# A six-layer attention and MLP stack on one core: where the normalised x and q are transposed

## The chip, the core and the metric

The kernel runs on one core of a Trainium2 chip. The metric is device time in microseconds (us). The core's engines are TensorE (PE: matmuls, and transpositions as matmuls against an identity), VectorE (DVE), ScalarE (ACT), GpSimd (POOL) and SyncE (SP), which here issues every DMA. On-chip memory is SBUF, 128 partitions wide; PE writes to PSUM, of which a tile here is one of 8 banks of 128 x 512 f32.

## The reference

The input x is (8, 1024, 128). With `mod = silu(c) @ wmod` cut into six vectors per batch element, the reference computes, in f32:

```python
h = layernorm(x) * (1 + ca) + sa
for i in range(6):
    xn = layernorm(h, ln1_w[i], ln1_b[i])
    q, k, v = heads(xn @ wq[i]), heads(xn @ wk[i]), heads(xn @ wv[i])   # 8 heads of 16
    context = softmax_over_tokens(k).T @ v
    h = (softmax_over_features(q) @ context) @ wo[i] + bo[i] + h
    xn = layernorm(h, ln2_w[i], ln2_b[i])
    h = leaky(xn @ w1[i]) @ w2[i] + h                                   # 128 -> 512 -> 128
x = x + ga * h
g = layernorm(x) * (1 + cb) + sb
x = x + gb * fp4_linear(silu(fp4_linear(g, w_gate)) * fp4_linear(g, w_up), w_down)
```

`fp4_linear` rounds both operands to a 4-bit grid in blocks of 16 and multiplies. The attention has no token-by-token matrix: `context` is 16 x 16 per head.

## The kernel before

**Layout.** One batch element b (1024 tokens of 128 features) is an SBUF tile of 128 partitions x 1024 columns: partition p holds tokens 8p to 8p + 7, each a chunk of 128 columns. It is worked in two halves (H = 2) of four chunks (HC = 4, HW = 512 columns). Matmuls contract over the partitions, so a projection needs its input with features on the partitions; that is what the transpositions are for.

**Lanes.** Four batch elements are in work at a time (LANES = 4). Lane b % 4 has its own set of big tiles, known by tags: X (the residual), A, B, C, D, E, and x0 (the original x). A tag is used again and again within a layer, and a new use waits for the last readers of the old one.

**A layer** (`layer`, L936), 48 times in all (8 batch elements x 6):

- `normed` (L919) for the attention: `layernorm` (L624) takes the statistics of each chunk (DVE, L640 and L646), 1/sqrt by a logarithm and an exponential (ACT, L660, L665) with one step of refinement (DVE, L670 to L686), and applies them: two chunks of a half on DVE (L692) and two on ACT (L699), into xh (tag A). `transposed` (L712) makes four PE transpositions into one PSUM bank (L718), and ACT takes the bank to xT (tag B) while it multiplies by the norm's weight and adds its bias, which are per-partition columns there (L928).
- k: one 512-column matmul per half with wk as the stationary operand (L948), maximum over tokens (DVE, L955), exponential with its sum (ACT, L971). q: four 128-column matmuls per half with a chunk of xT as the stationary operand (L995), softmax over features (DVE L1004, L1011, ACT L1018, DVE L1024, L1031), and the last multiplication on POOL (L1036), into tag D.
- k is transposed back (L718, copy on ACT at L1047), xh and k are multiplied into a 128 x 128 matrix (L1058), which goes through wv, a head mask and wo into m (L1067 to L1099).
- q is transposed (L718) and copied by ACT to qT (L1118, tag B); with its chunks as the stationary operand, m gives the attention's output (L1125), which DVE adds to x (L1110).
- `normed` for the MLP: xh in tag C, xT in tag A. Then four 512-column matmuls per half with w1 (L1171), the leaky activation on ACT (L1180), 16 128-column matmuls per half with chunks of the hidden tile as the stationary operand (L1188), and another addition on DVE (L1110).

After layer 6 of a batch element comes `ffn` (L1201): normalisation and modulation, fp4 rounding on DVE, ACT and POOL (`fp4`, L725), gate and up matmuls (L1232), fp4 again, transpositions (L1288), the down projection (L1312), and stores of x.

**The order.** No engine picks its own order. Every operation above is a step of a plan (`Plan`, L84) with an engine, an estimated duration, what it reads and writes, and a latency per engine until others see its result (`LAT`, L87: 2.6 us for SP). Steps marked `port` and all steps of POOL are kept apart in the plan (L174, L198). `order` (L143) simulates all engines and picks, at each moment, the step that can start first, and among equals the one with the longest tail of work behind it plus a lead. Leads stand in a table per batch element and stage (`LEAD`, L290: column 0 the start, 1 to 6 the layers, 7 the FFN), and `TURNS` (L301) changes single leads at given plan times. While the plan sees PE idle, it puts a matmul of the identity with itself in the gap (`warm`, L1358). The result is a fixed order per engine, which the engine then runs in sequence, each instruction waiting for its inputs. DMAs are steps of SP and stand in SP's order in the same way.

Of the kernel before, what the change touches and what calls it, by code (L numbers as in the profile page):

```python
# [11 lines left out]
ALU = mybir.AluOpType  # L12
# [219 lines left out]
    return 0.1 + n * 1.78e-3  # L232


def mm(n):

    return 0.0115 + n * 1.654e-3
# [5 lines left out]


TRANSPOSE = 0.109


@with_exitstack
def kernel(
# [38 lines left out]


    LEAD = [  # L290
        [2405, 3996, 461, 247, -1202, -1296, -1300, -3196],
        [1413, 1593, 3441, 1928, -2207, 1189, 1781, -248],
        [366, -108, -1676, -2703, -3835, 1594, -2630, -2514],
        [-241, 558, -1413, 208, -413, 228, -5405, -156],
        [694, -3633, -2192, -2384, -870, -487, -1194, -1272],
        [-3687, 2479, 1403, 3083, -1193, -6, -811, -1034],
        [725, 1777, 204, -1637, -400, -327, -320, -670],
        [3404, 589, 1158, 1867, -7, -962, -419, -2719],
    ]

    TURNS = [  # L301
        (3, [(1, 0, -62)]),
        (27, [(3, 0, -535)]),
        (36, [(2, 1, -485)]),
        (39, [(3, 1, -531)]),
        (45, [(0, 2, 1516), (2, 1, -553)]),
        (48, [(2, 1, -544)]),
        (57, [(1, 1, 1518), (1, 2, 2846), (1, 3, 649)]),
        (75, [(1, 1, 1516)]),
        (90, [(1, 1, 773)]),  # L310
        (105, [(0, 3, 2919), (0, 4, 1470), (0, 5, 1376), (0, 7, -524)]),
        (120, [(0, 3, 2762), (2, 1, -721)]),
        (150, [(1, 2, -201)]),
        (165, [(2, 1, 797)]),
        (180, [(1, 2, 1215)]),
        (210, [(2, 2, 832)]),
        (225, [(3, 1, 914), (3, 6, -4315)]),
        (240, [(0, 5, 828)]),
        (255, [(0, 5, 2639), (0, 6, 2635)]),
        (270, [(2, 3, 156)]),  # L320
        (285, [(0, 7, 811), (1, 3, 64)]),
        (300, [(4, 0, -33)]),
        (315, [(2, 2, 1013), (4, 0, 939)]),
        (330, [(3, 2, 544)]),
        (345, [(0, 7, 348), (2, 3, -400)]),
        (360, [(0, 7, 811), (2, 3, 1746), (2, 4, -2375)]),
        (405, [(1, 4, -3784), (4, 1, -3690)]),
        (420, [(1, 4, -3786)]),
        (435, [(2, 4, -3941)]),
        (450, [(1, 4, -2313)]),  # L330
        (465, [(4, 1, -4514)]),
        (480, [(1, 5, 1477)]),
        (495, [(3, 5, 1525)]),
        (525, [(1, 5, 1515), (2, 5, 1254)]),
        (555, [(1, 7, 1337)]),
        (570, [(2, 5, 1311)]),
        (600, [(1, 7, 1342)]),
        (615, [(1, 7, 1337), (3, 6, -3519), (5, 2, 2464)]),
        (630, [(3, 7, 1425)]),
        (675, [(5, 1, 2181)]),  # L340
        (690, [(4, 1, -2521)]),
        (705, [(2, 7, -2804), (4, 2, -2786), (4, 3, -4487), (4, 7, -1958)]),
        (735, [(5, 2, 3162)]),
        (780, [(6, 1, 323)]),
        (795, [(2, 7, -2027)]),
        (810, [(3, 7, 2088), (5, 3, 1769)]),
        (825, [(4, 3, -2043)]),
        (840, [(5, 4, -2386), (7, 1, 210), (7, 2, 779)]),
        (870, [(4, 3, -2494)]),
        (885, [(7, 1, 493)]),  # L350
        (915, [(6, 2, 913)]),
        (930, [(4, 3, -1826), (4, 4, -1241)]),
        (945, [(5, 4, -2139), (5, 6, -1878)]),
        (975, [(6, 3, -2917)]),
        (1005, [(7, 4, -2167)]),
        (1020, [(5, 5, -1207)]),
        (1035, [(5, 5, -1166)]),
        (1065, [(7, 4, -1977)]),
        (1140, [(4, 6, -2161), (5, 6, -1912)]),
        (1155, [(4, 6, -1857)]),  # L360
        (1170, [(4, 7, -1928)]),
        (1245, [(5, 7, -1905)]),
        (1260, [(6, 7, -139)]),
        (1275, [(6, 6, -1635)]),
        (1305, [(5, 7, -1974), (7, 7, 205)]),
        (1320, [(6, 7, -143), (7, 6, -143)]),
        (1335, [(6, 7, 201)]),
        (1350, [(6, 7, 206), (7, 7, 207)]),
    ]
    LATE = 140.0  # L370
    NQ = 4
# [337 lines left out]
        if HV:  # L709
            add("DVE", HV * 0.256, apply_v, r=[*at(src, h), mv, rstd], w=[low], port=True)  # L710

    def transposed(src, h):  # L712

        t = Ps(psum)

        def go():
            for c in range(HC):
                nc.tensor.transpose(  # L718
                    t.ap()[:, c * P : (c + 1) * P], chunks(half(src, h))[:, c, :], ident
                )  # L720

        add("PE", HC * TRANSPOSE, go, r=at(src, h), w=[t])
        return t

    def fp4(src, parts, ncol, n, i, last="POOL"):  # L725

# [189 lines left out]
            )  # L916


    def normed(ln, x, which, to, l, params, n):  # L919


        xh, xT = big(ln, which, f"xh_{n}"), big(ln, to, f"xT_{n}")
        for h in range(H):
            layernorm(ln, xh, x, h, n)
            t = transposed(xh, h)
            add(
                "ACT", act(HW, 2),
                lambda t=t, h=h: nc.scalar.activation(  # L928
                    half(xT, h), t.ap(), AF.Identity,
                    bias=col(params + 1, l), scale=col(params, l),  # L930
                ),
                r=[t, "cols"], w=at(xT, h),
            )
        return xh, xT

    def layer(x, b, l, ln, mod):  # L936
        n = f"{b}_{l}"
        xh, xT = normed(ln, x, "A", "B", l, 0, f"a{n}")

        nmax = Buf(lanes_p, [P, H + 1], f"nmax{ln}", f"nmax_{n}", H + 1)  # L940
        ksum = Buf(lanes_p, [P, H + 1], f"ksum{ln}", f"ksum_{n}", H + 1)
# [47 lines left out]
        for h in range(H):  # L989
            tq = Ps(psum)  # L990
            hs = slice(h * NH, (h + 1) * NH)

            def qmm(tq=tq, h=h):
                for c in range(HC):
                    nc.tensor.matmul(  # L995
                        tq.ap()[:, c * D : (c + 1) * D], half(xT, h)[:, c * P : (c + 1) * P],
                        wq_sb[:, l, :], start=True, stop=True,
                    )

            add("PE", HC * mm(D), qmm, r=[*at(xT, h), ("wq", l)], w=[tq])  # L1000

            add(
                "DVE", vec(HW),
                lambda tq=tq, hs=hs: nc.vector.tensor_reduce(  # L1004
                    qmax.ap()[:, hs], heads(tq.ap()), axis=AX.X, op=ALU.max
                ),
                r=[tq], w=[qmax[h]],
            )
            add(
                "DVE", vec(HW),  # L1010
                lambda tq=tq, h=h, hs=hs: nc.vector.tensor_tensor(  # L1011
                    heads(half(q, h)), heads(tq.ap()), each(qmax.ap()[:, hs]), ALU.subtract
                ),
                r=[tq, qmax[h]], w=at(q, h),
            )
            add(
                "ACT", act(HW) + 0.06,
                lambda h=h: nc.scalar.activation(half(q, h), half(q, h), AF.Exp),  # L1018
                w=at(q, h), func="exp",
            )  # L1020

            add(
                "DVE", vec(HW),
                lambda h=h, hs=hs: nc.vector.tensor_reduce(  # L1024
                    qsum.ap()[:, hs], heads(half(q, h)), axis=AX.X, op=ALU.add
                ),
                r=at(q, h), w=[qsum[h]],
            )
            add(
                "DVE", 0.25,  # L1030
                lambda hs=hs: nc.vector.reciprocal(qsum.ap()[:, hs], qsum.ap()[:, hs]),  # L1031
                w=[qsum[h]],
            )
            add(
                "POOL", pool2(HW) + 0.06,
                lambda h=h, hs=hs: nc.gpsimd.tensor_tensor(  # L1036
                    heads(half(q, h)), heads(half(q, h)), each(qsum.ap()[:, hs]), ALU.mult
                ),
                r=[qsum[h]], w=at(q, h),
            )  # L1040

        k = big(ln, "E", f"k_{n}")
        for h in range(H):
            t = transposed(kT, h)
            add(
                "ACT", act(HW),
                lambda t=t, h=h: nc.scalar.copy(half(k, h), t.ap()), r=[t], w=at(k, h),  # L1047
            )
# [53 lines left out]
            ),  # L1102
            r=[tc_, ksum[H], ("mb", l)], w=[m],
        )
        qT = big(ln, "B", f"qT_{n}")

        def onto_x(t, h):
            add(
# [3 lines left out]
            )  # L1112

        for h in range(H):
            t = transposed(q, h)
            add(
                "ACT", act(HW),
                lambda t=t, h=h: nc.scalar.copy(half(qT, h), t.ap()), r=[t], w=at(qT, h),  # L1118
            )
        for h in range(H):  # L1120
            to = Ps(psum)

            def out_mm(to=to, h=h):
                for c in range(HC):
                    nc.tensor.matmul(  # L1125
                        to.ap()[:, c * D : (c + 1) * D], half(qT, h)[:, c * P : (c + 1) * P],
                        m.ap(), start=True, stop=True,
                    )

            add("PE", HC * mm(D), out_mm, r=[*at(qT, h), m], w=[to])  # L1130
            onto_x(to, h)

        _, xmT = normed(ln, x, "C", "A", l, 2, f"m{n}")
        if l == L - 1:


# [24 lines left out]
        for h in range(H):  # L1161
# [23 lines left out]
            def ymm(ty=ty, hidden=hidden):  # L1185
                for c in range(HC):
                    for j in range(NJ):
                        nc.tensor.matmul(  # L1188
                            ty.ap()[:, c * D : (c + 1) * D], hidden(j)[:, c * P : (c + 1) * P],
                            w2g.ap()[:, j, :] if l == L - 1 else w2_sb[:, l, j, :],  # L1190
                            start=(j == 0), stop=(j == NJ - 1),
                        )
# [227 lines left out]
```

## Time and profile before

| | |
|---|---|
| median of 3 runs | 1400.22 us (1399.84 to 1400.36) |
| profiled execution, first to last instruction | 1398.7 us |
| PE busy / its weight loads | 1388.0 / 1115.6 us |
| DVE, ACT, POOL busy | 1136.0, 967.6, 250.4 us |
| transpositions of xh (attention), q, xh (MLP), k: instructions of each | 384 |
| evictions with weight and bias, L928 | 192, 0.777 us each |
| copies of qT, L1118 | 96, 0.586 us each |
| DMA issues of SP, bytes moved | 104, 18.79 MB |

The profiled execution's own time is given by its span, the first row's runs were not profiled; what lies around the span in a run is the difference of the two, 1.5 us. Durations in the table are medians of single records. A record holds the time until an instruction's result has landed, so records on one engine overlap: where the work is dense, what an instruction takes from its engine is the time from its start to the next one's start. An f32 matmul is recorded as two passes, each with its own weight load (PEld); a transposition is one. In lines of the timeline the columns are start, length, engine, line, operation, tiles and how many instructions were merged. "Idle before" an instruction is time of its engine only.

### The profile page before, as it was taken

What the parts mean: (1) busy time and instruction counts of PE and PEld (TensorE: products, weight loads), DVE (VectorE), ACT (ScalarE), POOL (GpSimd) and SP (SyncE); (2) the same over time, 40 slices, a digit from 0 to 9 for tenths busy, and PEclk for the clock granted to TensorE, in tenths of its full rate; (3) what the DMA queues carried; (4) which work ended last, traced back from release to release, by engine and by line L of the source; (5) the groups of instructions that cost most, each with busy time, mean ns of one, the idle gap of its engine ahead of it and who ended that gap; (6) DMA issues with size and microseconds to landing.
All of it is one profiled execution on the core that took longest, in us unless ns stands there. A gap on an engine that the chain in (4) does not pass through costs nothing. (4 is left out here: it accounts for less than half of the span.)

```text
span 1398.7 us, 26324 instructions
## 1 busy us (share of the span) xinstructions
PE 1388.0 (99%) x9181; PEld 1115.6 (80%) x9181; DVE 1136.0 (81%) x4504; ACT 967.6 (69%) x2284; POOL 250.4 (18%) x216
## 2 busy tenths in 40 slices
PE   9999999999999999999999999999999999999999
PEld 7779778877888887877887788787877887888877
DVE  8998747689878674999899999675767576899997
ACT  6886756676676765677768767676667667677674
POOL 2312000022201010223121241011010022222332
PEclk9999999999999999999999999999999999999999
DMA  7100000000000000000000000000000000000001
GB/s 219 47 1 1 1 1 1 1 17 12 16 1 1 1 1 1 16 13 20 27 12 13 1 31 1 1 1 1 1 1 1 0 1 1 2 1 1 16 8 39
DMA packets 16437, 18.79 MB, mean 13 GB/s; under 512 B 1600, under 2 KB 10536, under 8 KB 16304
## 3 DMA queue, kind: packets, MB, share of 16 engines
q1 hardware_dynamic: 16304, 17.10, 3.9%
q8 instruction: 73, 1.20, 0.4%
q14 instruction: 60, 0.49, 0.1%
HBM read 12.88 MB, written 4.22 MB: 12 GB/s over the span
## 5 line engine op out<-in xcount | busy, mean ns | idle before, releaser
L1171 PE MATMUL ps<-xT_m,w_sb 128*128 128x512 f32 x768 | 351.5, 593 | 1.3 <-ACT g L1240 0.9
L1171 PEld LDWEIGHTS ps<-xT_m,w_sb 128*128 128x128 f32 x768 | 136.3, 190 | 126.5 <-issue 90.4
L1036 POOL TENSOR_TENSOR q<-q,qsum 128x512 f32<-128x512 f32 x96 | 101.7, 1070 | 703.0 <-DVE qsum L1031 312.8
L1110 DVE TENSOR_TENSOR x<-ps,x 128x512 f32<-128x512 f32 x192 | 130.1, 681 | 111.9 <-PE ps L1188 96.6
L995 PEld LDWEIGHTS ps<-wq_sb,xT_a 128*128 128x128 f32 x768 | 96.3, 192 | 25.8 <-issue 16.3
L699 ACT ACTIVATE xh_a<-x,shift_a,rstd_a 128x128 f32<-128x128 f32 x192 | 83.4, 489 | 26.0 <-DVE shift_a L686 25.5
L1188 PEld LDWEIGHTS ps<-w_sb,hT_D 128*128 128x128 f32 x640 | 86.8, 192 | 15.8 <-issue 13.2
L995 PE MATMUL ps<-wq_sb,xT_a 128*128 128x128 f32 x768 | 98.6, 275 | 0.0
L1188 PE MATMUL ps<-w_sb,hT_E 128*128 128x128 f32 x640 | 97.6, 275 | 0.0
L1188 PE MATMUL ps<-w_sb,hT_C 128*128 128x128 f32 x640 | 97.6, 275 | 0.0
L1188 PE MATMUL ps<-w_sb,hT_B 128*128 128x128 f32 x640 | 97.6, 275 | 0.0
L1188 PE MATMUL ps<-w_sb,hT_D 128*128 128x128 f32 x640 | 97.5, 275 | 0.0
L1125 PEld LDWEIGHTS ps<-m,qT 128*128 128x128 f32 x768 | 91.4, 192 | 6.4 <-issue 1.4
L948 PE MATMUL ps<-xT_a,wk_sb 128*128 128x512 f32 x192 | 95.5, 596 | 0.5 <-DVE stats_a L640 0.3
L1058 PEld LDWEIGHTS ps<-k,xh_a 128*128 128x128 f32 x768 | 90.7, 192 | 6.4 <-issue 4.3
L1125 PE MATMUL ps<-m,qT 128*128 128x128 f32 x768 | 94.9, 275 | 0.0
L1058 PE MATMUL ps<-k,xh_a 128*128 128x128 f32 x768 | 93.4, 275 | 0.0
L699 ACT ACTIVATE xh_m<-x,shift_m,rstd_m 128x128 f32<-128x128 f32 x192 | 81.3, 487 | 17.3 <-DVE shift_m L686 17.1
L660 ACT ACTIVATE rstd_a<-mv_a,eps 128x4 f32<-128x4 f32 x96 | 28.4, 300 | 92.2 <-DVE mv_a L646 79.6
L640 DVE BATCH_NORM_STATS2 stats_a<-x 128x6 f32<-128x128 f32 x384 | 85.0, 278 | 1.6
L928 ACT ACTIVATE xT_m<-ps,cols 128x512 f32<-128x512 f32 x96 | 72.4, 777 | 19.9 <-PE ps L718 19.7
L1188 PEld LDWEIGHTS ps<-w_sb,hT_B 128*128 128x128 f32 x640 | 84.5, 192 | 0.7 <-issue 0.5
(181 smaller groups left out, 3217.8 us busy)
## 6 DMA issues: line engine op xcount, KB each, us to landing
x<-in_L_attn_x_dram SPq DMA_DIRECT2D x16, 256.0 KB, 3.2
out_dram<-x SPq DMA_DIRECT2D x14, 256.0 KB, 2.0
w_sb<-in_L_attn_w_dram SPq DMA_DIRECT2D x12, 256.0 KB, 4.5
mod<-mod_d SPq DMA_DIRECT2D x8, 256.0 KB
mod<-mod_d SPq DMA_DIRECT2D x4, 128.0 KB
out_dram<-x SPq DMA_DIRECT2D x4, 128.0 KB, 1.8
wk_sb<-in_L_attn_wk_dram SPq DMA_DIRECT2D x6, 64.0 KB, 3.4
wq_sb<-in_L_attn_wq_dram SPq DMA_DIRECT2D x6, 64.0 KB, 2.9
```

The lines of the kernel that those rows point to most:

```text
L640: "DVE", 0.197, lambda c=c: nc.vector.bn_stats(stats.ap()[:, c, :], s(c)),
L660: lambda: nc.scalar.activation(y(), var(), AF.Ln, bias=eps),
L699: nc.scalar.activation(d(c), s(c), AF.Identity, bias=shift.ap()[:, c : c + 1], scale=rstd.ap()[:, c : c + 1],)
L928: lambda t=t, h=h: nc.scalar.activation(half(xT, h), t.ap(), AF.Identity, bias=col(params + 1, l), scale=col(params, l),),
L948: lambda tk=tk, h=h: nc.tensor.matmul(tk.ap(), wk_sb[:, l, :], half(xT, h), start=True, stop=True),
L995: nc.tensor.matmul(tq.ap()[:, c * D : (c + 1) * D], half(xT, h)[:, c * P : (c + 1) * P], wq_sb[:, l, :], start=True, stop=True,)
L1036: lambda h=h, hs=hs: nc.gpsimd.tensor_tensor(heads(half(q, h)), heads(half(q, h)), each(qsum.ap()[:, hs]), ALU.mult),
L1058: nc.tensor.matmul(tc_.ap()[:, :D], chunks(xh.ap())[:, c, :], chunks(k.ap())[:, c, :], start=(c == 0), stop=(c == C - 1),)
L1110: lambda: nc.vector.tensor_tensor(half(x, h), t.ap(), half(x, h), ALU.add),
L1125: nc.tensor.matmul(to.ap()[:, c * D : (c + 1) * D], half(qT, h)[:, c * P : (c + 1) * P], m.ap(), start=True, stop=True,)
L1171: lambda th=th, h=h, j=j: nc.tensor.matmul(th.ap(), w1_sb[:, l, j * P : (j + 1) * P], half(xmT, h), start=True, stop=True,),
L1188: nc.tensor.matmul(ty.ap()[:, c * D : (c + 1) * D], hidden(j)[:, c * P : (c + 1) * P], w2g.ap()[:, j, :] if l == L - 1 else w2_sb[:, l, j, :],
```

## The change

For all layers but the first one of batch elements 0 to 3 (`dma = l > 0 or b >= LANES`), the transpositions of xh (attention), q and xh (MLP) go another way:

- one DVE instruction per half turns 32 x 32 blocks: partition block g keeps its partitions, and feature i*4 + f of token j of the block goes to partition i and column f*128 + j*4 + c (`turned`). It reads and writes with a step of four elements;
- four DMAs of SP, one per partition block, copy 32 partitions x 512 columns onto 128 partitions x 128 columns, in runs of 512 bytes, SBUF to SBUF, and finish the transposition: the column is now t*4 + c for token row t and chunk c;
- the norm's weight and bias, which ACT applied on the way out of PSUM, are applied in place on POOL (`tensor_scalar`); q has none.

The intermediate tile takes tag D before q, tag B for q, and tag B again for the MLP; the turned q is copied back into its own tile.

Columns within a half are therefore interleaved, t*4 + c in place of c*128 + t. Where PE takes one chunk's columns as the stationary operand (q, the transposition of k, the attention's output, the second MLP matmul) it now takes every fourth column (`each_chunk`).

In `normed`, in all 48 layers, the application of the statistics goes wholly to ACT (`layernorm(..., 0)`): four chunks of a half at L699, none at L692. `LEAD` and `TURNS` are replaced; the plan has three new constants for the new steps.

```diff
+def pool1(n):
+    return 0.1 + n * 1.2e-3
...
+TURN = 1.17e-3
+SQ = 32
...
     LEAD = [
-        [2405, 3996, 461, 247, -1202, -1296, -1300, -3196],
...
+        [6669, 6853, 111, 1873, 506, 0, 1316, 0],
...
     TURNS = [
-        (3, [(1, 0, -62)]),
...
+        (0, [(0, 1, 46), (0, 2, 3659), (2, 0, -210), (4, 6, 6661), (5, 2, -7325)]),
...
-    def transposed(src, h):
+    def each_chunk(t):
+        return t.rearrange("p (t c) -> p c t", c=HC)
+
+    def transposed(src, h, cut=chunks):
...
-                    t.ap()[:, c * P : (c + 1) * P], chunks(half(src, h))[:, c, :], ident
+                    t.ap()[:, c * P : (c + 1) * P], cut(half(src, h))[:, c, :], ident
...
+    def turned(src, via, dst, h):
+        add(
+            "DVE", TURN * HC * D,
+            lambda: nc.vector.transpose(
+                half(via, h).rearrange("p (f j c) -> p c f j", f=P // SQ, c=HC),
+                half(src, h).rearrange("p (c i f) -> p c f i", f=P // SQ, c=HC),
+            ),
+            r=at(src, h), w=at(via, h),
+        )
+
+        def spread():
+            for g in range(P // SQ):
+                nc.sync.dma_start(
+                    half(dst, h)[:, g * P : (g + 1) * P],
+                    half(via, h)[g * SQ : (g + 1) * SQ, :],
+                )
+
+        add("SP", P // SQ * 0.48, spread, r=at(via, h), w=at(dst, h))
...
-    def normed(ln, x, which, to, l, params, n):
+    def normed(ln, x, which, via, to, l, params, n, dma):
         xh, xT = big(ln, which, f"xh_{n}"), big(ln, to, f"xT_{n}")
+        y = big(ln, via, f"y_{n}") if dma else None
         for h in range(H):
-            layernorm(ln, xh, x, h, n)
-            t = transposed(xh, h)
-            add("ACT", act(HW, 2), ...)
+            layernorm(ln, xh, x, h, n, 0)
+            if not dma:
...
+                continue
+            turned(xh, y, xT, h)
+            add(
+                "POOL", pool1(HW),
+                lambda h=h: nc.gpsimd.tensor_scalar(
+                    half(xT, h), half(xT, h), col(params, l), col(params + 1, l),
+                    ALU.mult, ALU.add,
+                ),
+                r=["cols"], w=at(xT, h),
+            )
...
-        xh, xT = normed(ln, x, "A", "B", l, 0, f"a{n}")
+        dma = l > 0 or b >= LANES
+        cut = each_chunk if dma else chunks
+        xh, xT = normed(ln, x, "A", "D", "B", l, 0, f"a{n}", dma)
...
-                        tq.ap()[:, c * D : (c + 1) * D], half(xT, h)[:, c * P : (c + 1) * P],
+                        tq.ap()[:, c * D : (c + 1) * D], cut(half(xT, h))[:, c, :],
...
-            t = transposed(kT, h)
+            t = transposed(kT, h, cut)
...
-        qT = big(ln, "B", f"qT_{n}")
+        y = big(ln, "B", f"yq_{n}")
+        qT = q if dma else y
...
+            if dma:
+                turned(q, y, q, h)
+                continue
...
-                        to.ap()[:, c * D : (c + 1) * D], half(qT, h)[:, c * P : (c + 1) * P],
+                        to.ap()[:, c * D : (c + 1) * D], cut(half(qT, h))[:, c, :],
...
-        _, xmT = normed(ln, x, "C", "A", l, 2, f"m{n}")
+        _, xmT = normed(ln, x, "C", "B", "A", l, 2, f"m{n}", dma)
...
-                            ty.ap()[:, c * D : (c + 1) * D], hidden(j)[:, c * P : (c + 1) * P],
+                            ty.ap()[:, c * D : (c + 1) * D], cut(hidden(j))[:, c, :],
```

## The prediction

> **What bounds the kernel now.** I read the busy table first, then the 100 us windows, the timeline, the groups by line and the DMA issues.
>
> ```profile
> span 1398.7 us, 26324 instructions
> PE 1388.0 (99%) x9181; PEld 1115.6 (80%) x9181; DVE 1136.0 (81%) x4504; ACT 967.6 (69%) x2284; POOL 250.4 (18%) x216
> ...
> PE 38%; DVE 2%; ACT 0%; issue 0%; POOL 0%; ACTq 0%
> ```
>
> TensorE (PE) is busy for 1388 of 1398.7 us. The chain that ended last is followed back over two fifths of the span, and 38 of its 40 hundredths are PE. VectorE (DVE) is next at 81%. The filler matmuls of L1360 are 24.3 us of PE's time (174 instructions) and lie in the first 50 and the last 50 us, so between those PE is full of real work. The windows (start:length, then PE, PEld, DVE, ACT, POOL) say what happens when DVE is crowded too:
>
> ```profile
> 0.00:100.00 100.00, 95.35 (x616) 75.66 (x617) 94.04 (x464) 75.67 (x206) 25.76 (x31) 1.00 0.31 94
> ...
> 700.00:800.00 100.00, 100.00 (x645) 79.83 (x644) 92.77 (x340) 72.57 (x164) 23.62 (x19) 1.00 0.04 9
> ...
> 1000.00:1100.00 100.00, 100.00 (x640) 77.64 (x640) 63.63 (x268) 65.82 (x151) 8.40 (x8) 1.00 0.00 1
> ```
>
> With DVE at 93% PE still had no gap; DVE's other 19% is slack. So PE work taken away is time gained, until another engine is the later one. The clock was 1.00 throughout.
>
> What PE pays is the distance between starts, not the record, since records overlap:
>
> ```profile
> 699.65 0.60 PE L718 MATMUL ps<-ident,xh_a 128*128 128x128 f32 x4
> 700.09 0.61 PE L1188 MATMUL ps<-w2g,hT_B 128*128 128x128 f32 x4
> 700.53 0.61 PE L1188 MATMUL ps<-w2g,hT_C 128*128 128x128 f32 x4
> ```
>
> Four transpositions take 700.09 - 699.65 = 0.44 us, 0.109 each. A 128-column matmul is two passes of 0.111.
>
> **PE.** 44 of the 48 layers change (the first layer of lanes 0 to 3 does not), with two halves and three turns (xh for attention, q, xh for the MLP): 264 turns, each in place of four transpositions. 1056 x 0.109 = 115.1 us leave PE.
>
> **ACT.** Removed: 176 evictions of L928 at 0.663 us from start to start (116.7) and 88 copies of L1118 at 0.477 (42.0). Added: the other half of the norm's application, 384 chunks of L699 at 0.385 (147.8; all 48 layers). Net -11 us of 968: no change.
>
> **DVE.** The same 384 chunks leave L692: 98 us at the usual 0.256 from start to start, 121.5 with the stalls in its records; I take 110. The 264 turns of 128x512 come in.
>
> ```profile
> 699.59 0.68 DVE L903 TENSOR_TENSOR h<-h,mod 128x512 f32<-128x512 f32 x1
> 700.18 0.87 DVE L640 BATCH_NORM_STATS2 stats_a<-x 128x6 f32<-128x128 f32 x4
> 700.97 0.36 DVE L646 BATCH_NORM_AGGREGATE mv_a<-stats_a 128x2 f32<-128x6 f32 x4
> ```
>
> No row shows a turn, or a DVE stream that steps 16 bytes. The lower end is the ordinary 512-column operation, 700.18 - 699.59 = 0.59. The upper end is the slower statistics, 0.79 for four times 128 columns. An instruction can't cost less than nothing, and a gain is excluded. I take 0.60, the row of the same shape: 264 x 0.60 = 158 (upper end 209). DVE becomes 1136 - 110 + 158 = 1184 us (upper end 1235).
>
> A rule speaks against this. The Trainium skill, "VectorE: DVE Perf Modes", section "Rules for kernel authors", says to transpose 128x128 on TensorE where PSUM will do, and section "The three transpose paths" gives 390 ns there against 311 on VectorE, in bf16 and 32x32 blocks only. The trace's 0.109 in a stream is far under 390. An estimate by the page's 311 for each of four chunks is 1.24 us a turn and DVE at 1353, which would leave almost no gain.
>
> **POOL.** 176 scale-and-shift operations on 128x512 that ACT did in its eviction. Lower end: the memset of 768 columns took 0.742, so 0.50. Upper end: the two-input multiply, L1036, 1.07. I take 0.9, nearer the upper as the only 512-column row: 158 us, POOL 408, a third of the span. Behind one that waits stand the q multiplies (L1036), the FFN's L791 and the adds of L911, whose readers are DVE and PE. L692 went up to 1.3 us beside POOL work; fewer DVE chunks and more POOL work about cancel there.
>
> **SP and the copies.** Each turn issues four copies of 64 KB: 1056.
>
> ```profile
> 25.25 0.43 SPq L426 DMA_DIRECT2D wq_sb<-in_L_attn_wq_dram  x1
> 25.73 0.43 SPq L426 DMA_DIRECT2D wv_sb<-in_L_attn_wv_dram  x1
> ```
>
> The issues by line give the time to landing at the end:
>
> ```profile
> out_dram<-x SPq DMA_DIRECT2D x14, 256.0 KB, 2.0
> ...
> wq_sb<-in_L_attn_wq_dram SPq DMA_DIRECT2D x6, 64.0 KB, 2.9
> ```
>
> One issue takes 0.475 (25.73 - 25.25): 1056 x 0.475 = 502 us of SP, which has only 104 issues now. Packets of 512 bytes took 28.7 ns on average (7648 in the trace): 1056 x 128 x 28.7 / 16 = 242 us on each DMA engine, under a fifth of the span. Neither is a bound. On SP a turn that waits for DVE holds back the other lanes' copies, the loads of x and the stores.
>
> **Latency.** Before, xh to xT was 0.44 + 0.78 (eviction record) = 1.2 us. After: 0.60 for the turn, 3 x 0.475 until the fourth issue, 2.0 to 2.9 to land (no row copies SBUF to SBUF; I take 2.9), 0.9 on POOL: 5.8, so +4.6. q has no POOL step behind the copy: 4.9 against 1.0, +3.9. The cover is the time that data now wait for PE. As means over 96 halves, from the end of the eviction to the start of the first matmul, that is 2.5 us (xT for k), 6.5 (xT for w1) and 6.6 (qT). Two of three are covered; the first lacks 2.1. Four independent lanes share PE, so in the rewritten order another lane's matmul can stand there. If none did, 88 x 2.1 = 185 us would come back.
>
> **PE's strided weights.** Because columns now lie as t*4+c, the weight loads of the q, output and second MLP matmuls (48 per layer, two passes each: 4224 passes) and of k's transpositions (352) step 16 bytes. No row steps so. Loads now:
>
> ```profile
> 699.54 0.47 PEld L718 LDWEIGHTS ps<-ident,xh_a 128*128 128x128 f32 x4
> 699.98 0.53 PEld L1188 LDWEIGHTS ps<-w2g,hT_B 128*128 128x128 f32 x4
> ```
>
> A load takes 0.141 for a transposition and 0.192 for a matmul, and starts with the pass before it. The lower end is nothing, if the step is free (a gain is excluded: no column fewer is loaded). The upper end by rows is the spread of the two, 0.051 on each of 4576 passes: 233 us. I take nothing: every load is started a whole pass ahead, and both kinds keep the 0.11 between starts.
>
> The Trainium skill speaks against this too: "SBUF — State Buffer", "Specifications (TRN2)", has 16-byte lines that need two hits each for full speed, and here every element is on a new line. With the 128 / 1.2 = 107 ns that "TensorE: Matmul & The Clock Gate", "LDWEIGHTS", gives a load, halving the rate is an estimate of 4224 x 0.10 = 430 us more. No run here shows it.
>
> **The sum.** 1398.7 - 115.1 = 1283.6 if PE stays full. DVE would stand at 1184 / 1284 = 92%, as in the window 700:800, where PE lost nothing, and under the 94% of 0:100, where it lost 5% (start-up loads included). I take 2%, 26 us. Span 1309.6. The median of the runs, 1400.22, lies 1.5 above the profiled span, so the time is **1311**. Its own range is 1278 (no loss; POOL and DVE at their lower ends) to 1335 (4% loss).
>
> **The rivals.**
>
> *DVE or the copies come last* (0.27). For: DVE at 92% in the mean must go above that beside an FFN, whose windows already show 92 to 93%; and a third of the 185 us above is 62. Against: PE's fullness at 93%. With turns at 0.79, DVE's 1235 at 92% is 1342, so about 1345; with a third of the stalls, about 1350 as well. The turn cancels the gain from about 1.1 us (1026 + 264 x 1.1 = 1316, 94% of 1400); 0.02 of the chance lies near there, 0.07 beyond it.
>
> *Strided weight loads slow PE* (0.18), the case that ends slower. The place is the 48 matmuls per layer of L995, L1125 and L1188, the price up to 233 us: 1283.6 + 233 + 1.5 = 1518. It decides from 115 / 4576 = 25 ns per pass. For: nothing hides a load that outlasts its pass, and these are half of PE's time. Against: each is started a pass ahead, and a transposition's load, as many columns, takes only 0.141.
>
> *More than the sum* (0.02): under 1278, if DVE's lost stalls free PE as well.
>
> **Numbers.** Likeliest case 0.53. Faster: 0.53 + 0.02 + 0.18 of the first rival = 0.73. Same (within 0.2%, about what a measurement of this kernel can tell): 0.02 + 0.01 = 0.03. Slower: 0.07 + 0.17 = 0.24. The range runs from 1278 to 1455: it holds the likeliest case, nearly all of the first rival, and the second where the loads cost up to 37 ns. Some 0.16 lies outside.
>
> **What would show it.** PE: 1056 transpositions fewer, those that are left at 0.109; q, output and second MLP passes still 0.111 from start to start (the second rival: longer there, PE still at 99%). DVE: turns of 0.60 from start to start, busy about 1184. SP: four issues a turn, landing under 3 us. First rival: PE's idle time grows and is ended by POOL's xT or DVE. I am wrong on the mechanism if a strided pass is longer, and on the size if PE waits over 50 us.

## The result and the profile after

The changed kernel takes 1890.16 us in the median (1887.1 to 1890.86, 4 runs), the kernel before 1400.29 beside it (1399.84 to 1400.75). The ratio is 1.349, 95% interval 1.347 to 1.351: 490 us slower, where the forecast was 89 us faster. The profiled span is 1888.3 us, with a mean granted clock of 0.99. The head of the page and the first line of its chain:

```profile
span 1888.3 us, 28098 instructions
...
PE 1858.2 (98%) x8651; PEld 1585.5 (84%) x8651; DVE 1313.8 (70%) x4384; ACT 972.2 (51%) x2412; POOL 390.6 (21%) x392
...
PE 87%; DVE 8%; ACT 2%; issue 1%; DMA 1%; SPq 1%; POOL 1%; DVEq 0%; POOLq 0%; ACTq 0%
```

PE is about as full as before (98% for 99%), with 530 instructions fewer, and has 470 us more of work. So nearly all of the time went into longer instructions and not into waiting. The 100 us windows of the prediction (columns as there) say the same:

```profile
0.00:100.00 100.00, 95.60 (x618) 79.11 (x619) 87.01 (x412) 77.24 (x215) 28.87 (x35) 1.00 0.36 104
700.00:800.00 100.00, 98.51 (x452) 85.10 (x452) 71.59 (x231) 51.39 (x123) 24.56 (x22) 1.00 0.14 36
1000.00:1100.00 100.00, 99.31 (x500) 88.97 (x500) 70.38 (x240) 48.50 (x126) 21.40 (x22) 1.00 0.21 48
```

From 1000 to 1100 us PE is 99% busy, but with 500 matmul records where there were 640. Which ones grew, the timeline of PE shows (start, length):

```profile
757.51 1.10 PE L1266 MATMUL ps<-w_sb,hT_B 128*128 128x128 f32 x4
758.45 1.10 PE L1266 MATMUL ps<-w_sb,hT_C 128*128 128x128 f32 x4
759.38 1.10 PE L1266 MATMUL ps<-w_sb,hT_B 128*128 128x128 f32 x4
```

Four passes of the second MLP matmul now take 758.45 - 757.51 = 0.94 us; before it was 0.44. As medians from start to start over the whole trace, a pass with a strided stationary operand takes 0.233 us instead of 0.112, at all three places (L1069, L1203, L1266); k's transposition 0.120 instead of 0.109; a pass whose operand lies side by side 0.112, as before. The groups by line show it as weight loads, and show the turn:

```profile
L1069 PEld LDWEIGHTS ps<-wq_sb,xT_a 128*128 128x128 f32 x768 | 179.2, 316 | 11.4 <-issue 5.5 <-PE ps L1069 0.7 <-DVE shift_a L710 0.2
...
L1203 PEld LDWEIGHTS ps<-m,q 128*128 128x128 f32 x704 | 169.2, 328 | 12.5 <-DVE m L1173 5.6 <-issue 4.2 <-DVE stats_a L675 1.0
...
L1266 PEld LDWEIGHTS ps<-w_sb,hT_C 128*128 128x128 f32 x640 | 156.8, 316 | 0.0
L769 DVE STREAM_TRANSPOSE y_a<-xh_a 128x512 f32<-128x512 f32 x88 | 100.4, 1143 | 27.7 <-ACT xh_a L734 27.7
...
L1438 PE MATMUL warm<-ident 128*128 128x128 f32 x700 | 96.7, 282 | 2.4 <-POOL ident masks.py:199 1.6 <-DVE g L1326 0.5
...
L1000 POOL TENSOR_SCALAR xT_a<-xT_a,cols 128x512 f32<-128x512 f32 x88 | 70.3, 799 | 435.8 <-DMA xT_a<-y_a 339.9 <-PE ps L1203 40.2 <-ACT rstd_a L700 27.8
```

The fourth field is busy time and the mean of one record: loads of 328 ns where all are strided (316 where the four first layers, which do not change, are in the mean; 192 before), turns of 1143 ns, GpSimd operations of 799 ns, and 700 filler records where there were 174.

The sum of these terms closes: 1398.7 - 115 (1056 transpositions) + 511 (4224 strided passes x 0.121) + 4 (352 of k x 0.011) + 72 (fillers, 24.3 to 96.7) + 19 (PE's idle, 10.7 to 30.1) = 1890, against a span of 1888.3.

### The profile page after: what moved, and what is told of

Same layout as the page of the kernel before. It is cut to its first block, busy times and chain, and to the rows that moved or that the text cites. A ratio compares the mean times of both kernels' runs of the same rounds, so it can differ in the third digit from the quotient of the medians.

```text
span 1888.3 us, 28098 instructions
## 1 busy us (share of the span) xinstructions
PE 1858.2 (98%) x8651; PEld 1585.5 (84%) x8651; DVE 1313.8 (70%) x4384; ACT 972.2 (51%) x2412; POOL 390.6 (21%) x392
## 3 DMA queue, kind: packets, MB, share of 16 engines
q8 instruction: 70, 1.15, 0.3%
## 4 chain that ended last, share of the span: by engine, by line
PE 87%; DVE 8%; ACT 2%; issue 1%; DMA 1%; SPq 1%; POOL 1%; DVEq 0%; POOLq 0%; ACTq 0%
PE ps L1266 35%; PE ps L1249 16%; PE ps L1203 9%; PE ps L1069 8%; PE ps L1022 4%; PE ps L1132 4%; PE ps L757 2%; PE ps L1310 2%; PE warm L1438 2%; PE ps L1390 2%; PE ps L1366 1%; SPq L778 1%; ACT xh_a L734 1%; PE ps L1166 1%; DVE yq L769 1%
## 5 line engine op out<-in xcount | busy, mean ns | idle before, releaser
L1069 PEld LDWEIGHTS ps<-wq_sb,xT_a 128*128 128x128 f32 x768 | 179.2, 316 | 11.4 <-issue 5.5
L1203 PEld LDWEIGHTS ps<-m,q 128*128 128x128 f32 x704 | 169.2, 328 | 12.5 <-DVE m L1173 5.6
L1069 PE MATMUL ps<-wq_sb,xT_a 128*128 128x128 f32 x768 | 179.2, 383 | 0.0
L734 ACT ACTIVATE xh_a<-x,shift_a,rstd_a 128x128 f32<-128x128 f32 x384 | 157.3, 483 | 41.1 <-DVE shift_a L721 35.1
L1203 PE MATMUL ps<-m,q 128*128 128x128 f32 x704 | 171.6, 396 | 2.7 <-issue 1.4
L734 ACT ACTIVATE xh_m<-x,shift_m,rstd_m 128x128 f32<-128x128 f32 x384 | 155.4, 484 | 27.4 <-DVE shift_m L721 27.0
L1266 PE MATMUL ps<-w_sb,hT_E 128*128 128x128 f32 x640 | 167.9, 385 | 0.0
L1266 PE MATMUL ps<-w_sb,hT_C 128*128 128x128 f32 x640 | 167.9, 385 | 0.0
L1266 PE MATMUL ps<-w_sb,hT_B 128*128 128x128 f32 x640 | 167.0, 384 | 0.0
L1266 PEld LDWEIGHTS ps<-w_sb,hT_D 128*128 128x128 f32 x640 | 158.3, 314 | 10.3 <-issue 4.5
L1266 PE MATMUL ps<-w_sb,hT_D 128*128 128x128 f32 x640 | 164.6, 380 | 0.0
L1266 PEld LDWEIGHTS ps<-w_sb,hT_B 128*128 128x128 f32 x640 | 157.2, 315 | 3.0 <-issue 1.9
L1266 PEld LDWEIGHTS ps<-w_sb,hT_E 128*128 128x128 f32 x640 | 156.9, 316 | 0.0
L1266 PEld LDWEIGHTS ps<-w_sb,hT_C 128*128 128x128 f32 x640 | 156.8, 316 | 0.0
```

Source lines behind the costliest of these rows:

```text
L734: nc.scalar.activation(d(c), s(c), AF.Identity, bias=shift.ap()[:, c : c + 1], scale=rstd.ap()[:, c : c + 1],)
L1069: nc.tensor.matmul(tq.ap()[:, c * D : (c + 1) * D], cut(half(xT, h))[:, c, :], wq_sb[:, l, :], start=True, stop=True,)
L1203: nc.tensor.matmul(to.ap()[:, c * D : (c + 1) * D], cut(half(qT, h))[:, c, :], m.ap(), start=True, stop=True,)
L1266: nc.tensor.matmul(ty.ap()[:, c * D : (c + 1) * D], cut(hidden(j))[:, c, :], w2g.ap()[:, j, :] if l == L - 1 else w2_sb[:, l, j, :], start ...
```

## The experiments

Two theories for the step at first. **A**: the step of 16 bytes of the stationary operand makes each weight load, and with it each pass, longer. **B**: PE's operand reads suffer from what the change adds beside them, the copies above all. And a question behind both: does the forecast hold without the step?

**e1_contig.** The change with stationary operands side by side; the copies, turns and order stay.

```diff
-        cut = each_chunk if dma else chunks
+        cut = chunks
```

> The changed kernel with one edit: PE takes each chunk's 128 columns side by side again where the change takes every fourth one (the tokens come out in another order, so the output is not the reference's; turns, copies, POOL work and the order of all engines stay). Theory A (the step of 16 bytes slows the weight loads): the passes of the q, output and second MLP matmuls go from 0.233 us back to 0.112, 4224 x 0.121 = 511 us less, about 1380 us, DVE near 94% of the span. Rival B (PE is slow because of the copies or the traffic beside it): the passes stay near 0.233 and the time near 1890. Rival C (passes recover, but DVE, whose turns take 1.07 us, or the copies end last): passes 0.112, PE idle or on filler matmuls for over 100 us, time 1420 to 1500.

1456.63 us (1451.64 to 1459.86), ratio 1.039 (1.036 to 1.042). Passes are back at 0.112 with the copies still there, as theory A has it, and 434 of the 490 us are gone. But the rest is slower than the kernel before, not faster. Head and chain of the page:

```profile
span 1456.4 us, 27949 instructions
...
PE 1379.6 (95%) x8651; PEld 1076.3 (74%) x8651; DVE 1293.5 (89%) x4384; ACT 966.5 (66%) x2412; POOL 391.7 (27%) x392
...
DVE 48%; PE 30%; ACT 7%; DMA 5%; SPq 4%; issue 3%; POOL 2%; DVEq 0%; ACTq 0%; POOLq 0%
```

Now VectorE leads the chain, and the copies' queue and landing stand in it with 9 hundredths.

**e2_before_step4** and **e3_before_mixed**: the kernel before, with nothing added but the step of the stationary operand, by `every(t, c, s)`, which takes 128 columns with step s. In e2 it is 4 at q, k's transposition, the output and the second MLP matmul. In e3 it is 2 at q and k, 3 at the output, 1 at the MLP.

```diff
-                        tq.ap()[:, c * D : (c + 1) * D], half(xT, h)[:, c * P : (c + 1) * P],
+                        tq.ap()[:, c * D : (c + 1) * D], every(half(xT, h), c, 4),
```

> The kernel before with one edit: the stationary operands of q, the transposition of k, the attention's output and the second MLP matmul take every fourth column, in all 48 layers (a part of the computation is permuted, the output is not the reference's). No turn, no copy, no other order. Theory A: 4608 passes at 0.233 in place of 0.112 (558 us) and 384 transpositions at 0.120 in place of 0.109 (4 us): about 1960 us. Rival B (copies or traffic slow the loads): no change, 1400 us, passes at 0.112.

> The kernel before with steps of its own per line: q takes every second column (8 bytes), the attention's output every third (12 bytes), the transposition of k every second, the second MLP matmul stays at one (a part of the computation is permuted, the output is not the reference's). If a step costs as the lines of 16 bytes say, two hits in a line are enough: q passes stay at 0.112, the output's go up (4/3 hits a line) to between 0.15 and 0.23, and the time is 1430 to 1490. If any step costs the whole price: q and output at 0.233, 1536 x 0.121 = 186 us, about 1586. If only 16 bytes do: 1400.

e2 took 1946.25 us (one run), with passes of 0.233 and no copy or turn in the kernel: theory B falls. Two of its groups of four passes, and the output's loads:

```profile
699.88 1.10 PE L1194 MATMUL ps<-w_sb,hT_B 128*128 128x128 f32 x4
700.81 1.10 PE L1194 MATMUL ps<-w_sb,hT_C 128*128 128x128 f32 x4
```

```profile
L1131 PEld LDWEIGHTS ps<-m,qT 128*128 128x128 f32 x768 | 184.3, 328 | 5.0 <-DVE m L1105 0.9 <-ACT xT_m L934 0.5 <-ACT xh_m L699 0.5
```

e3 took 1453.25 (one run). Its weight loads by line (the output with step 3, q with 2, the MLP with 1, k with 2):

```profile
L1131 PEld LDWEIGHTS ps<-m,qT 128*128 128x128 f32 x768 | 139.2, 261 | 5.6 <-issue 1.1 <-DVE m L1105 0.9 <-ACT xT_m L934 0.5
...
L1001 PEld LDWEIGHTS ps<-wq_sb,xT_a 128*128 128x128 f32 x768 | 101.0, 196 | 25.5 <-issue 16.2 <-PE ps L1001 1.9 <-PE ps L954 1.4
...
L1194 PEld LDWEIGHTS ps<-w_sb,hT_D 128*128 128x128 f32 x640 | 86.9, 192 | 15.8 <-issue 12.4 <-ACT hT_B L1186 1.2 <-ACT k L1053 0.2
...
L724 PEld LDWEIGHTS ps<-ident,kT 128*128 128x128 f32 x384 | 52.0, 206 | 7.1 <-issue 3.7 <-ACT kT L977 2.1 <-DVE stats_i L640 0.2
```

From start to start a matmul's pass takes 0.112 us at step 1, 0.118 at 2, 0.174 at 3 and, in e2, 0.233 at 4. A step of 8 bytes is nearly free for it, one of 16 doubles the pass. k's transposition does not follow this: it takes 0.120 at step 2 and 0.121 at step 4 (0.109 at 1), and its load grows from 141 ns to 206 already at step 2.

**e4_turns** and **e5_free**: e1 with the turn's step taken away too. In e4 the attention's turn reads and writes side by side, the MLP's still reads with the step, q's still writes with it. In e5 all three are side by side; the edit below is e5's.

```diff
-                half(via, h).rearrange("p (f j c) -> p c f j", f=P // SQ, c=HC),
-                half(src, h).rearrange("p (c i f) -> p c f i", f=P // SQ, c=HC),
+                half(via, h).rearrange("p (c f j) -> p c f j", f=P // SQ, c=HC),
+                half(src, h).rearrange("p (c f i) -> p c f i", f=P // SQ, c=HC),
```

> E1 with three kinds of turn (data come out in another order): xh of the attention reads and writes side by side, xh of the MLP reads every fourth column and writes side by side, q reads side by side and writes every fourth (now all read and write with a step of four and take 1.07 us from start to start, 1.14 as records). Theory A2 (the turn itself takes two cycles an element): all three keep 1.14. Theory A3 (the step costs, as on PE): the first takes about 0.68 (0.60 from start to start); the second and third show which side costs, 1.14 or 0.68. Time under A3: DVE loses 88 to 264 x 0.47 us, 40 to 120, and the kernel 0 to 60 us against E1.

> E1 with turns that read and write side by side in all three places (blocks of 32 come out in another order, so the output is not the reference's): neither PE nor DVE steps 16 bytes any more; order, copies and POOL work are those of the changed kernel. The prediction's sum without the two steps is 1311. Theory D (what is left in E1 over that sum is DVE, which ends last): turns at 0.70 a record take another 79 us off DVE's busy time against E4, and the time falls from 1427 by about 0.75 of that, to 1365 to 1375. Theory L (the copies' latency and the order, which has filler matmuls written into it, hold PE up): DVE's relief helps little more, 1395 to 1415, with PE's 700 fillers and its idle time as in E4.

e4 took 1426.89 us (one run). Its turns:

```profile
L771 DVE STREAM_TRANSPOSE y_m<-xh_m 128x512 f32<-128x512 f32 x88 | 97.6, 1110 | 22.7 <-ACT xh_m L734 20.6 <-DMA xT_a<-y_a 1.5 <-DMA q<-yq 0.2
...
L771 DVE STREAM_TRANSPOSE yq<-q 128x512 f32<-128x512 f32 x88 | 97.4, 1122 | 3.1 <-POOL q L1112 2.8
...
L771 DVE STREAM_TRANSPOSE y_a<-xh_a 128x512 f32<-128x512 f32 x88 | 61.7, 702 | 25.7 <-ACT xh_a L734 25.6
```

The step on either side alone costs nearly the price of both. From start to start a turn takes 0.625 us side by side, 0.96 when only written with the step, 1.03 when read with it (1.02 to 1.03 in the change). e5 took 1407.64 (1405.44 to 1409.39), ratio 1.005 (1.003 to 1.007), with these busy times:

```profile
PE 1357.2 (97%) x8651; PEld 1072.7 (76%) x8651; DVE 1197.5 (85%) x4384; ACT 963.6 (69%) x2412; POOL 389.9 (28%) x392
```

So even with no step anywhere the change gives nothing: 97 us lie between e5 and the forecast's 1311.

**e7_no_copies, e8_no_fillers, e9_neither** ask what those are made of, with e5's order of all steps kept.

```diff
-                half(via, h).rearrange("p (c f j) -> p c f j", f=P // SQ, c=HC),
+                half(src, h).rearrange("p (c f j) -> p c f j", f=P // SQ, c=HC),
...
-        add("SP", P // SQ * 0.48, spread, r=at(via, h), w=at(dst, h))
+        add("SP", P // SQ * 0.48, lambda: None, r=at(via, h), w=at(dst, h))
...
-                    half(xT, h), half(xT, h), col(params, l), col(params + 1, l),
+                    half(xT, h), half(xh, h), col(params, l), col(params + 1, l),
```

(e7 and e9; in e8 and e9 the plan leaves a gap without a filler after its first 60 us.)

> The kernel of e5_free without its 1056 copies: the turns work in place, GpSimd reads the turned half directly and writes xT, the output matmul reads the turned q directly. The order on every engine and the 700 filler records stay as they are, so no step stands elsewhere. (Left out: the copies, so the result is not the reference's.) e5_free took 1407.6 with PE's records at 1357 of 1405.7, 97 of that fillers. If the copies' way (three further issues, 2.1 us to landing) makes PE wait: PE's idle 48 us falls below 20, time 1365 to 1380. If VectorE's load or the fixed order makes it wait: no change, 1398 to 1410.

> The kernel of e5_free without the filler matmuls after the first 60 us of the plan (568 of 700 records, about 79 us of PE's busy time); nothing else stands elsewhere. If fillers only fill waits that are there anyway: time 1400 to 1410, PE's idle grows from 48 to about 125 us. If fillers are themselves in the way, because real work is ready earlier than the plan thought: up to 79 us less, 1330 to 1390. The granted clock shows whether gaps cost clock: it stays at 1.00 if they do not.

> e7 and e8 together: no copies and no fillers after the first 60 us, order as in e5_free (result not the reference's). The PE work left is about 1260 + 18 us. If copies and fillers are what separates e5_free from the sum of the prediction (1311): 1285 to 1330. If VectorE (1197 us busy in e5_free) or the order still makes PE wait: 1345 to 1400.

e7: 1378.61 (1378.02 to 1380.41); e8: 1411.0 (1410.58 to 1411.67); e9: 1380.8 (1378.8 to 1381.68). Busy times of e7, then of e8:

```profile
PE 1347.8 (98%) x8651; PEld 1066.8 (77%) x8651; DVE 1190.7 (87%) x4384; ACT 962.2 (70%) x2412; POOL 387.9 (28%) x392
```

```profile
PE 1312.7 (93%) x8083; PEld 1014.5 (72%) x8083; DVE 1195.7 (85%) x4384; ACT 963.0 (68%) x2412; POOL 391.0 (28%) x392
```

The copies' way is worth 29 us. Leaving the fillers out gains nothing: e8 is 3 us slower than e5. PE idles for 96.1 us in place of 48.5, and its other records take 1293.7 us (1312.7 less the 19.0 of the fillers that stay) in place of 1260.2 (1357.2 less 97.0), with a mean granted clock of 0.978 for 0.993. So the fillers stand for the most part where PE would wait anyway. Whether some of them also hold up work that is ready is not shown, because the lower clock changes the same sum.

**e6_short_runs.** The change done in full without any step: the turn side by side on both sides, the copies in runs of 128 bytes to the right place, and the order of features that follows taken up by row-permuted loads of wk, wq and w1, in layers 1 to 5 of all batch elements. Leads as in the change.

```diff
-                half(via, h).rearrange("p (f j c) -> p c f j", f=P // SQ, c=HC),
-                half(src, h).rearrange("p (c i f) -> p c f i", f=P // SQ, c=HC),
+                half(via, h).rearrange("p (f c j) -> p c f j", f=P // SQ, c=HC),
+                half(src, h).rearrange("p (c f i) -> p c f i", f=P // SQ, c=HC),
...
-                    half(dst, h)[:, g * P : (g + 1) * P],
+                    chunks(half(dst, h))[:, :, g * SQ : (g + 1) * SQ],
```

> A kernel that computes the whole reference with turns in layers 2 to 6 of every batch element and no step of 16 bytes anywhere: the turn reads and writes side by side, the copies write runs of 128 bytes in place of 512 (four times as many packets), columns come out in their plain order, and the features' order on the partitions (i*4 + f for feature f*32 + i) is met by loading wk, wq and w1 in that row order and by permuting wk's columns, the head mask and the norm's columns once. Leads are those of the changed kernel, which were not made for it. Theory: turns 0.70 a record, passes 0.112, copies land within 4 us in spite of the short runs; the time itself is set by the order and lies between 1400 and 1480. Rival: 540 thousand packets of 128 bytes fill the DMA engines (over 60% of their time) and the landings go over 6 us, 1500 or more.

1479.62 us (one run); passes 0.112, turns 0.625, copies landing after 2.4 us (2.1 in the change), but 1168 filler records. Without the fillers' 159.5 us PE is busy for 1268.3 us (1363.7 before), so its real work fell and its planned waits grew. That the order, made for other steps, is to blame is what e12 tests.

**e12_order_all, e10_order_mlp_q, e11_order_q, e15_order_attention, e16_order_mlp** have e6's steps, with leads and turns of the plan searched anew for each and the plan's duration of a turn and of a copy's issue set to the measured ones, and differ in the sites that are turned. **e13_order_free** and **e14_order_contig** do the same to e5 and e1 (there only the turn's duration is set). The edit is shown against e6.

```diff
     LEAD = [
-        [6669, 6853, 111, 1873, 506, 0, 1316, 0],
+        ...
```

> A complete kernel: the way of e6 (side-by-side turns, copies in runs of 128 bytes, no step anywhere) for q and for the MLP's norm only, in layers 1 to 5 (160 turns); the attention's norm keeps its transpositions and evictions. Leads and turns of the order are searched anew for these steps, with the durations that e5 and e6 showed (turn 0.62, copy issue 0.67). Removed from PE: 160 x 4 x 0.109 = 70 us. If the order, not the design, is what held e5_free and e6 back: 1340 to 1375. If VectorE and the copies make PE wait in any order: at least 1395.

> The same for q alone (80 turns in layers 1 to 5), with its own searched order. Removed from PE: 80 x 4 x 0.109 = 35 us, and 80 copies of 0.48 from ScalarE. The sum with PE full is 1365; with an order made for it 1365 to 1385, if each copy's way shows at PE in any order 1400 or more.

> The steps of e6 (1479.6) with an order searched anew for them, nothing else changed. If e6 lost its time to an order that was not made for it: 1385 to 1420. If three turns per half are too much for VectorE and SyncE whatever the order: within 20 us of 1480.

> The steps of e5_free (1407.6; turns side by side, no strided operand on TensorE, result not the reference's) with leads and turns of the order searched anew for the durations that were measured (turn 0.625). Nothing else is changed. If the order, which was not made for these durations, holds e5_free back: 1370 to 1395, and the 700 filler records fall. If the turns and copies cost this in any order: 1400 to 1410.

> The steps of e1_contig (1456.6; the turns as in the change at 1.03, stationary operands side by side, result not the reference's), with an order searched anew for a turn of 1.03. If the order is what kept e1 behind the kernel before: 1390 to 1425. If VectorE (1293 us busy) sets it in any order: 1440 to 1460.

> A complete kernel like e11_order_q, with the turn, the copies and the GpSimd step at the attention's norm alone (80 turns, layers 1 to 5) and its own searched order. Removed from PE: 80 x 4 x 0.109 = 35 us; the sum with PE full is 1365, as for q alone (e11: 1382.5). The prediction gave this site the shortest cover, 2.5 us between the eviction and k's matmul against 6.5. If a short cover is what costs: 1395 to 1420, above e11 by more than 10. If the sites cost alike: 1375 to 1390.

> The same at the MLP's norm alone (80 turns, layers 1 to 5), its own searched order, sum with PE full 1365. Cover 6.5 us, as long as q's, but with the GpSimd step and the strided-free copies of e10. If cover decides: 1370 to 1390, near e11 and at least 10 below e15. If the GpSimd step decides: near e15.

| sites turned | run | us, median | ratio (95%) | span | 1398.7 less the transpositions | above it |
|---|---|---|---|---|---|---|
| q | e11 | 1382.49 | 0.987 (0.986 to 0.989) | 1380.3 | 1364 | 16 |
| MLP | e16 | 1389.18 | 0.992 (0.990 to 0.993) | 1387.6 | 1364 | 24 |
| attention | e15 | 1417.51 | 1.012 (1.010 to 1.013) | 1416.1 | 1364 | 52 |
| q, MLP | e10 | 1355.4 | 0.968 (0.966 to 0.969) | 1353.3 | 1329 | 24 |
| all three | e12 | 1403.6 | 1.002 (1.001 to 1.003) | 1402.2 | 1294 | 108 |

(320 transpositions of 0.109 us per site.) The heads of e10, e15 and e12:

```profile
PE 1341.2 (99%) x8696; PEld 1064.6 (79%) x8696; DVE 1185.5 (88%) x4506; ACT 947.9 (70%) x2292; POOL 318.1 (24%) x307
```

```profile
PE 1398.8 (99%) x9168; PEld 1119.5 (79%) x9168; DVE 1146.1 (81%) x4426; ACT 976.4 (69%) x2368; POOL 310.2 (22%) x297
```

```profile
PE 1372.1 (98%) x8836; PEld 1086.1 (77%) x8836; DVE 1195.7 (85%) x4426; ACT 957.0 (68%) x2370; POOL 385.2 (27%) x387
```

e10 beats both kernels, by 45 us and by 535. VectorE is busier in it (1185.5 us, 88%) than in e15 (1146.1, 81%), which is slower, and only 10 us less busy than in e12 (1195.7, 85%), so VectorE's load as such is not what costs there. Adding the attention's norm to e10 takes 35 us from PE and makes it 48 slower; alone it is the one site that loses. In e15 the fillers took 67.3 us, against 24.3 before. 167 of its 480 filler records (25.6 us) lie between 50 and 1300 us, where the kernel before has none; the others lie at the start and the end, where fewer lanes are in work (174 before). q alone (e11) has 22 in that stretch, the MLP alone (e16) 62, e10 118, e12 436. In e15 none of these stand directly ahead of k's matmul, which reads the turned data; the longest stretches stand ahead of w1's matmul (5.8 us in all), the transpositions of the MLP's norm (4.7) and the output (4.6). So it is shown that this site loses, but not by which wait.

The order matters: e6 to e12, same steps, 76 us; e1 to e14 (1440.24), 16 us, though e14's order changes no single leads at plan times (`TURNS` is empty), as the others do. For e5 it gave nothing (e13: 1407.79), so there the order was not the cause, as far as the search went; a longer one could still move any of these by some us.

## Why the prediction was wrong

**The step that failed**, as the prediction put it: "I take nothing: every load is started a whole pass ahead, and both kinds keep the 0.11 between starts." A strided load's record is 0.137 us longer (329 ns for 192), and the pass takes 0.121 more: 4224 x 0.121 = 511 us, more than the whole change was worth at best. Two things went wrong in it. First, being started a pass ahead did not hide the longer loads: e2 alters nothing but the step of what is loaded, and the passes go to 0.233 with it. Both kinds in the trace before stood at 0.11, so it could not be told whether passes or loads set that pace; the row was read as slack. Second, the upper end, 0.051, was the spread of two loads that both read side by side, with nothing in it of a step: the true price was 2.4 times what was called a bound. The second rival (strided weight loads slow PE) had the place and the mechanism right and less than half of the price, 233 us for 511; the range ended at 1455 because of it.

The prediction cited the Trainium skill, "SBUF — State Buffer", section "Specifications (TRN2)", on two hits per 16-byte line. The measured passes bear that out for the matmuls' stationary operands: 0.118 with two f32 on a line, 0.233 with one. k's transposition does not fit it: 0.120 with two, 0.121 with one. The estimate from it, 430 us, was 81 below the measured 511.

The other terms, one by one:

- *115.1 us of transpositions leave PE*: right; 1056 fewer, and the sum in the section on the result closes with it.
- *k's transpositions*: the load grew (141 to 207 ns) but the pass only from 0.109 to 0.120. Why a transposition suffers so much less than a matmul pass was not tried.
- *A turn of 0.60, at most 0.79*: 0.625 side by side, which is the row it was taken from, and 1.03 as the change has it. The step was named as what no row shows, and then bounded by rows without a step, the same error as on PE. VectorE came to 1313.8, not 1184; in e5, without the step, to 1197.5. The turn's step costs e1 49 us against e5.
- *ScalarE net nothing*: right, 967.6 to 972.2. *GpSimd 0.9 a step*: 0.80, and 390.6 in all for 408. L1036 was not the only row of 512 columns (L791 took 1.15, L911 up to 1.42); the result lies below them all.
- *Copies*: an issue took more than the 0.475 of the loads, as SP's queue shows; 5.07 / 8 = 0.63. They land after 2.1 us. Packets of 512 bytes took 34.9 ns in place of 28.7, so the copies took about 295 us (1056 x 128 x 34.9 / 16) of each DMA engine and not 242, still far from a bound.

```profile
709.01 5.07 SPq L778 DMA_DIRECT2D xT_m<-y_m  x8
```

- *Latency of 5.8 us in place of 1.2*: 1.03 + 3 x 0.63 + 2.1 + 0.80 = 5.8, right in the sum by errors that cancel.
- *"Two of three are covered; the first lacks 2.1"*: it fits what came. The attention's norm, with 2.5 us of cover, loses 52 us where q and the MLP's norm, with 6.6 and 6.5, lose 16 and 24. That the cover is the reason is argued from these three sites, each in an order of its own. *"Another lane's matmul can stand there"* was the optimistic half of that step: in e12 no order was found in which it stands there.
- *A loss of 2% (26 us)*: mis-sized. Without any step it is 123 us, as e5 lies 97 above the 1311 that has these 26 in it. Of the 97, 29 are the copies' way (e7); leaving out the fillers (e8, e9) or a new search of the order (e13) gave none back. The 68 that are left were not split further; e15 and e12 put most of the loss at the attention's norm. The first rival (VectorE or the copies last, 1345) comes nearest to it and was 63 too low; of its two causes e7 shows the copies.
- *A range of its own from 1278*: its sum without any loss is 1283.6 + 1.5 = 1285, and no term gives the 7 us below that.

## What to carry to other kernels

Where a change alters the access pattern of an operand that already streams at its pace, the rows of unstrided work do not bound its cost. Keep both ends open until a small kernel that changes the pattern alone has shown it, as e2 does in one line. Move PE's transpositions away one site at a time: the same replacement gained 45 us at two sites and lost it all with the third. Here the two were those where the data wait longest for PE.

## What the runs showed of the hardware

- f32 matmul passes of 128 columns, by the step of the stationary operand's columns: 4 bytes 0.112 us, 8 bytes 0.118, 12 bytes 0.174, 16 bytes 0.233. A one-pass transposition: 0.109 at 4 bytes, 0.120 at 8, 0.121 at 16 (e2).
- A 32 x 32 turn of 128 x 512 f32 on VectorE: 0.625 us side by side; 0.96 with a step of 16 bytes in the writes, 1.03 in the reads, 1.02 to 1.03 in both. The two do not add.
- SBUF to SBUF copies of 64 KB landed after 2.1 us in runs of 512 bytes, after 2.4 in runs of 128.
- With more gaps in PE's work the granted clock was lower: 0.978 in the mean without fillers (e8), with PE idle for 1408.8 - 1312.7 = 96 us, against 0.993 with them (e5), idle for 48.5.
